# A two-layer mixture-of-experts kernel: five of eight batches stored among the last sparse tiles, sums pinned behind the last output, eight output buffers, and an end in program order

## The chip, the cores and the metric

The kernel runs on one core of a Trainium2 chip, as one program and one launch. The metric is the device time in microseconds (us). Before the change it is 367.66 us, the median of three runs (367.42 to 375.38).

One core has a matrix engine (TensorE, "PE" in the profile; its weight loads are listed apart as "PEld"), a vector engine (VectorE, "DVE"), an engine for activation functions (ScalarE, "ACT"), GpSimd ("POOL"), and SyncE ("SP"), which here does nothing but issue DMAs and wait. Each engine has its own stream of instructions and runs it in order; engines wait for each other at semaphores. DMAs can be issued from SyncE, ScalarE and GpSimd, and their packets are moved by sixteen DMA engines.

## The reference

The input `x` is 8 batches of 256 tokens with 128 features, in f32. Two layers run on it, each with a residual:

```python
x = x + L0_ffn(L0_cond(x, ..., prompt_type))    # pooling, then 8 experts, dense
x = x + L1_ffn(L1_cond(x, ..., language))       # adapter, then top 2 of 8 experts
```

`L0_cond` gives every position an attention-pooled sum over its batch: scores are `tanh(x W1 + b1) . v`, masked by one of three masks that depend on the batch's prompt type, and then a softmax. `L0_ffn` runs all eight experts on every token (128 to 512, gelu with tanh, back to 128) and sums them with gates; a gate is the logit where it is at least the 3072nd smallest of all logits, and else 0.

`L1_cond` is a small adapter per language (128 to 32, relu, back), a residual, and a layer norm with a scale and shift per language. `L1_ffn` is the part that matters here:

```python
xn = layernorm(x) * gamma + beta
probs = softmax(xn @ gate_w)                     # 8 experts
w, idx = top_k(probs, 2);  w = w / sum(w)
out_e = gelu(xn @ w1[e] + b1[e]) @ w2[e] + b2[e] # 128 -> 512 -> 128
return sum_e(w_e * out_e) + x                    # two experts per token
```

So every token has exactly two rows of expert output, and the result of a token is its residual plus these two rows.

## The kernel before

**Tiles.** The 2048 tokens are 16 token tiles of 128 (two for each batch), in four groups of four. The work is cut into five units (`UNITS`): units 0 to 2 have four token tiles each, units 3 and 4 two each.

**The dense layer.** `layer("first", ...)` runs unit by unit and expert by expert: first matmuls (L784), gelu on ScalarE (L786), second matmuls (L764), gating and accumulation on VectorE (L752, L754). Its weights `w10` lie in a pool called `first` under the tag `w1`, with eight buffers; its second weights `w20` lie in the pool `const`. Between matmuls, `pump()` advances generators, which write the other work's instructions in among them.

**Routing.** When a unit's dense layer is finished, its `adapt(u)` is put behind as such a generator. It computes the adapter and norms, keeps the residual in `resid`, picks the two experts of each token, and counts rows by expert through two small matmuls with the constant `ones` and a triangle (`kp`). From these it takes each row's position, and GpSimd writes each token's normalized row, together with its destination number and its weight, twice into a scratch tensor `xs` in device memory by an indirect DMA (L676). In `xs` every expert has a region of its own, so each expert's rows lie one behind the other.

**Lists.** After units 2, 3 and 4 (`SLOTS = {2: 17, 3: 21, 4: 39}`) VectorE turns the counts into a list of 128-row tiles: `tiles_of` (how many tiles each expert has: full ones, at the end also the begun ones), `cumulated` and `listed` (for slot k: which expert, and which row of `xs`). `used` remembers how many tiles of each expert were already listed, and the list of the next unit goes on from there. Slots 0 to 16 come from the first list, 17 to 20 from the second, 21 to 38 from the third. Which rows are in which tile depends on the data, so the kernel learns the tile's start and expert from the list at run time.

**The sparse layer.** For each slot k there are four steps:

- `fetch`: SyncE reads the slot's row and expert from the list into registers, and loads the 128 rows `xt` from `xs` (L814) and the expert's first weights `wt`, 256 KB (L822).
- `turn`: TensorE transposes (L829), VectorE scales (`xc`, L831) and copies the expert's bias (`b1`, L833).
- `hidden`: four matmuls (L840) and four gelus on ScalarE (L842) into `hs`, in a ring of 15 buffers under the tag `scr`.
- `output`: four matmuls (L849), bias on VectorE into `yt` (L852, four buffers), the row's weight on ScalarE (L853), and on GpSimd an indirect DMA of the 128 rows into the second scratch tensor `ys` (L854), to the destination that each row carries.

The steps of different slots overlap: fetches run five slots ahead (`LEAD`), the others two (`AHEAD`). Slots up to `SURE` = 36 always run; slots 36 to 38 stand under a `tc.If` on the count of tiles (L903 to L905), and were not taken in the profiled execution.

**The end** (L906 to L916). Row numbers in `ys` are `(p n t s)`: partition, batch, half of the batch's tokens, first or second expert. Each batch's rows, 256 KB, are read back, alternately from SyncE's and ScalarE's queue; VectorE adds the first row to the residual and the second to that; and the sum is stored, 128 KB for each batch, from the same two queues:

```python
for n in range(B):
    yg.append(work.tile([P, 2, 2 * D], F32, tag="scr", name=f"yg{n}", bufs=NSCR))
    (nc.scalar if n % 2 else nc.sync).dma_start(out=yg[n], in_=yv[n])
for n in range(B):
    ...
    nc.vector.tensor_tensor(o, yg[n][:, :, :D], resid[...], ALU.add)
    nc.vector.tensor_tensor(o, o, yg[n][:, :, D:], ALU.add)
    (nc.scalar if n % 2 else nc.sync).dma_start(out=of[n], in_=...)
```

**What sets the order.** The framework's scheduler orders the instructions of each engine, with the place in the program as priority, and puts in the waits between engines from what reads and writes the same buffer or tensor. Where the program knows better, it says so: `declare_no_dep` with a named group takes away the dependence of one DMA on a group of others, as the output scatters have among themselves. No such thing is said of the scatters and the reads of the end, so every read of `ys` stands behind every scatter.

Of the kernel before, what the change touches and what calls it, by code (L numbers as in the profile page):

```python
# [22 lines left out]
P = 128  # L23
# [19 lines left out]
SURE = 36  # L43
NOWHERE = 1 << 20
# [24 lines left out]
def tile_adaln_ffn_d2(ctx: ExitStack, tc: tile.TileContext, x, ptype, lang, cols, b1v,  # L69
# [36 lines left out]
    for e in range(E):  # L106
        t = first.tile([P, HC * P], F32, tag="w1", name=f"w10_{e}")
        nc.sync.dma_start(out=t, in_=w10[e])
        w10s.append(t)
        t = const.tile([P, HC, D], F32, name=f"w20_{e}")  # L110
        nc.sync.dma_start(out=t, in_=w20[e])
        w20s.append(t)
# [5 lines left out]
    nc.gpsimd.memset(ones, 1.0)  # L118
# [242 lines left out]
    nc.gpsimd.iota(dest, pattern=[[1, 2], [2, NT]], base=0, channel_multiplier=2 * NT)  # L361
# [140 lines left out]
    used = const.tile([P, E], F32, name="used")  # L502
    nc.gpsimd.memset(used, 0.0)
# [15 lines left out]
    def cumulated(f, name):  # L519
        c3 = small.tile([P, E, E], F32, tag="c3", name=f"c3_{name}", bufs=2)  # L520
        nc.vector.tensor_tensor(c3, upto, f.unsqueeze(1).to_broadcast([P, E, E]), ALU.mult)
        cf = small.tile([P, E], F32, tag="cf", name=f"cf_{name}")
        nc.vector.tensor_reduce(cf, c3, AX.X, ALU.add)
        return cf

    def tiles_of(counts, edges, name):

        c2 = small.tile([P, E, NT], F32, tag="c2", name=f"c2_{name}", bufs=2)
        nc.vector.tensor_tensor(c2, counts.unsqueeze(2).to_broadcast([P, E, NT]),
                                edges.unsqueeze(1).to_broadcast([P, E, NT]), ALU.is_ge)  # L530
        f = small.tile([P, E], F32, tag="f", name=f"nf_{name}")
# [3 lines left out]
    def listed(f, cf, first, k0, k1, name):  # L535
# [3 lines left out]
        shape = [P, n, E]  # L539
        past = small.tile(shape, F32, tag="past", name=f"past_{name}", bufs=1)  # L540
        nc.vector.tensor_tensor(past, kth[:, :n].unsqueeze(2).to_broadcast(shape),
                                cf.unsqueeze(1).to_broadcast(shape), ALU.is_ge)
        ek = small.tile([P, n], F32, tag="ek", name=f"ek_{name}", bufs=1)
        nc.vector.tensor_reduce(ek, past, AX.X, ALU.add)

        step = small.tile([P, E], F32, tag="step", name=f"step_{name}", bufs=1)
        if first is None:
            nc.vector.tensor_copy(step, f)
        else:
            nc.vector.tensor_tensor(step[:, :E - 1], first[:, :E - 1], first[:, 1:], ALU.subtract)  # L550
            nc.vector.tensor_copy(step[:, E - 1:], first[:, E - 1:])
            nc.vector.tensor_tensor(step, step, f, ALU.add)
# [4 lines left out]
        if first is not None:  # L557
            nc.vector.tensor_scalar(row, row, first[:, 0:1], None, ALU.add)  # L558
# [7 lines left out]
    def adapt(u, acc):  # L566
# [99 lines left out]
        if u in SLOTS:  # L666
            counts = small.tile([P, E], F32, tag="counts", name=f"counts{u}", bufs=2)
            nc.vector.tensor_copy(counts, kp[:, nt, :])
        for s, oh in enumerate((oh1, oh2)):
# [17 lines left out]
        if u in SLOTS:  # L687
# [3 lines left out]
            if lists:  # L691
# [275 lines left out]
```

## Time and profile before

The profile is of one execution. It took 380.68 us, with a span of 379.0 us from its first to its last instruction and a mean granted TensorE clock of 0.977 of full speed; the median of the three runs without profile is 367.66 us.

| | busy us | share of span | instructions |
|---|---|---|---|
| PE (matmuls) | 345.8 | 91% | 1596 |
| PEld (weight loads) | 233.0 | 61% | 1596 |
| DVE | 195.0 | 51% | 801 |
| ACT | 167.0 | 44% | 387 |
| POOL | 94.5 | 25% | 142 |

DMA moved 46.12 MB in 33,603 packets, 122 GB/s over the span.

The dense layer's matmuls (L784 and L764) take 241.8 us of PE's 345.8, the sparse layer's (L840 and L849) 78.8. The profile names groups by source line, by the program's tile names (`ys<-yt,xt` is a scatter of outputs, `yg<-ys` a read at the end, `xt<-xs` and `wt<-in_w_dram` the fetches) and by shape. A row of the timeline gives the start of a stretch, its length, the engine, the line and tiles, the number of instructions in it, and in brackets how long the engine had been idle before it and what it waited for. "SPq" and "ACTq" are the sequencers that issue DMAs. In the profile's page the span is also cut into 40 slices of 9.5 us, and each digit is the busy share of a slice in tenths.

### The profile page before, as it was taken

How to read it: one execution, taken by the hardware profiler on the slowest of the kernel's cores; microseconds unless marked ns; L12 is line 12 of the kernel's file. 1: busy time of each engine (PE TensorE's matmuls, PEld its weight loads, DVE VectorE, ACT ScalarE, POOL GpSimd, SP SyncE). 2: the span in 40 equal slices, each digit the busy share in tenths (PEclk: the TensorE clock that was granted, in tenths of full speed). 3: DMA queues.
4: the chain of work that ended last, by engine and by line, in shares of the span. 5: the costliest groups of instructions: out<-in, count | busy, mean ns of one | idle time of the engine just before them, and what ended most of it. 6: DMA issues, size and time to landing. Idle time of an engine off the chain costs nothing. (4 is left out here: it accounts for less than half of the span.)

```text
span 379.0 us, 5911 instructions
## 1 busy us (share of the span) xinstructions
PE 345.8 (91%) x1596; PEld 233.0 (61%) x1596; DVE 195.0 (51%) x801; ACT 167.0 (44%) x387; POOL 94.5 (25%) x142
## 2 busy tenths in 40 slices
PE   6799999999999999999999999989989879999900
PEld 6695444444444445445445688857869769999900
DVE  4775565542245675565512474847576644333305
ACT  2166434553542244223443244425635637567800
POOL 8100000000000030650350021262045565444530
PEclk9999999999999999999999999999999998999975
DMA  6935999005222101210130001126543554566136
GB/s 189 382 84 150 368 379 356 4 0 148 69 77 102 56 30 55 63 49 30 56 69 14 28 29 42 36 65 175 151 121 107 162 162 121 168 187 173 47 117 244
DMA packets 33603, 46.12 MB, mean 122 GB/s; under 512 B 5349, under 2 KB 16375, under 8 KB 33569
## 3 DMA queue, kind: packets, MB, share of 16 engines
q1 hardware_dynamic: 29024, 39.26, 34.6%
q0 software_dynamic: 2304, 4.37, 3.2%
q10 hardware_dynamic: 2240, 2.10, 1.6%
q8 instruction: 14, 0.23, 0.3%
q14 instruction: 21, 0.16, 0.1%
HBM read 31.57 MB, written 14.39 MB: 121 GB/s over the span
## 5 line engine op out<-in xcount | busy, mean ns | idle before, releaser
L786 ACT ACTIVATE hT_first<-hp_first,col 128x512 f32<-128x512 f32 (+1 forms) x160 | 93.4, 601 | 103.3 <-PE hp_first L784 102.3
L784 PE MATMUL hp_first<-poolT,w 128*128 128x512 f32 (+1 forms) x320 | 121.2, 513 | 1.3 <-DVE xr L591 0.7
L764 PE MATMUL yp_first<-hT_first,w 128*128 128x512 f32 (+1 forms) x320 | 120.6, 511 | 0.0
L784 PEld LDWEIGHTS hp_first<-poolT,w 128*128 128x128 f32 x320 | 58.8, 190 | 44.2 <-issue 38.2
L764 PEld LDWEIGHTS yp_first<-hT_first,w 128*128 128x128 f32 x320 | 59.0, 190 | 42.5 <-issue 38.6
L676 POOL DMA_INDIRECT xs<-zr,pos x32 | 31.5, 986 | 64.3 <-DVE pos L674 27.9
L842 ACT ACTIVATE hs<-hps,b 128x128 f32<-128x128 f32 x144 | 40.6, 365 | 11.2 <-PE hps L840 5.3
L854 POOL DMA_INDIRECT ys<-yt,xt x36 | 35.2, 977 | 40.9 <-ACT hs L842 28.3
L849 PE MATMUL yps<-w,hs 128*128 x288 | 39.6, 283 | 2.5 <-DVE row L558 2.4
L840 PE MATMUL hps<-xc,wt 128*128 128x128 f32 x288 | 39.2, 280 | 1.1 <-issue 1.1
L849 PEld LDWEIGHTS yps<-w,hs 128*128 128x128 f32 x288 | 35.7, 195 | 4.3 <-issue 3.5
L752 DVE SCALAR_TENSOR_TENSOR part_first<-yp_first,col,gbc_first 128x512 f32<-128x512 f32 (+1 forms) x28 | 17.2, 614 | 40.4 <-PE yp_first L764 39.9
L840 PEld LDWEIGHTS hps<-xc,wt 128*128 128x128 f32 x288 | 36.0, 196 | 0.8 <-issue 0.6
L853 ACT ACTIVATE yt<-yt,xt 128x128 f32<-128x128 f32 x36 | 14.6, 405 | 23.3 <-issue 15.0
L754 DVE TENSOR_TENSOR acc_first<-acc_first,part_first 128x512 f32<-128x512 f32 (+1 forms) x35 | 20.1, 580 | 0.5
L579 POOL MEMSET ha<- 1x512 f32 x5 | 2.6, 516 | 67.6 <-PE dp L588 67.4
L406 POOL DMA_DIRECT2D gd_L<-gT_L x1 | 0.6, 649 | 74.3 <-DVE gT_L L404 74.3
L833 DVE COPY b<-col 128x4 f32 x36 | 7.2, 200 | 23.0 <-ACT hs L842 17.7
L852 DVE TENSOR_TENSOR yt<-yps,b2all 128x128 f32<-128x128 f32 x36 | 10.5, 291 | 14.8 <-PE yps L849 7.1
L831 DVE TENSOR_SCALAR xc<-xtp,col 128x128 f32<-128x128 f32 x36 | 14.4, 401 | 4.0 <-PE xtp L829 2.4
L772 ACT ACTIVATE y_first<-yp_first,col 128x512 f32<-128x512 f32 x8 | 5.5, 687 | 24.2 <-PE yp_first L764 24.2
L420 DVE TENSOR_SCALAR_CACHE_REDUCE fl<-logit,tr 128x128 f32<-128x128 f32 x46 | 13.5, 343 | 0.6
(205 smaller groups left out, 304.2 us busy)
## 6 DMA issues: line engine op xcount, KB each, us to landing
wt<-in_w_dram SPq DMA_DIRECT2D x36, 256.0 KB
xs<-empty SPq DMA_DIRECT2D x1, 8580.0 KB
w<-in_w_dram SPq DMA_DIRECT2D x24, 256.0 KB
gbc_first<-gd_L SPq DMA_DIRECT2D x24, 256.0 KB
xt<-xs SPq DMA_DIRECT2D x36, 65.0 KB
gbc_first<-gd_L SPq DMA_DIRECT2D x16, 128.0 KB
lgb<-in_lgb_dram SPq DMA_DIRECT2D x8, 128.0 KB
yg<-ys ACTq DMA_DIRECT2D x4, 256.0 KB
```

The costliest lines, as they stand in the source:

```text
L676: move = nc.gpsimd.indirect_dma_start(out=xs, out_offset=bass.IndirectOffsetOnAxis(ap=pos[:, t:t + 1], axis=0), in_=zr[s][:, t, :], in_off ...
L752: nc.vector.scalar_tensor_tensor(part, y, bias, gbc, ALU.add, ALU.mult)
L754: nc.vector.tensor_tensor(accs[u], accs[u], part, ALU.add)
L764: nc.tensor.matmul(yp, lhsT=w2s[e][:, c, :], rhs=hT[:, c, :], start=(c == 0), stop=(c == HC - 1))
L784: nc.tensor.matmul(hp, lhsT=w1s[e][:, c * P:(c + 1) * P], rhs=sources[g][:, o * P:o * P + n], start=True, stop=True)
L786: nc.scalar.activation(hT[:, c, :], hp, act, bias=col[:, cb1 + e * HC + c:cb1 + e * HC + c + 1])
L831: nc.vector.tensor_scalar(xc, tp, col[:, C_LG:C_LG + 1], col[:, C_LB:C_LB + 1], ALU.mult, ALU.add)
L840: nc.tensor.matmul(hp[:, c, :], lhsT=wt[:, c * P:(c + 1) * P], rhs=xc, start=True, stop=True)
L842: nc.scalar.activation(hT[:, c, :], hp[:, c, :], AF.Gelu, bias=b1[:, c:c + 1])
L849: nc.tensor.matmul(yp, lhsT=hT[:, c, :], rhs=w21[:, bass.ds(ek, 1), c * D:(c + 1) * D], start=(c == 0), stop=(c == HC - 1))
L853: nc.scalar.activation(yt, yt, AF.Copy, scale=xt[:, D + 1:D + 2])
L854: move = nc.gpsimd.indirect_dma_start(out=ys, out_offset=bass.IndirectOffsetOnAxis(ap=xt.bitcast(I32)[:, D:D + 1], axis=0), in_=yt, in_off ...
```

## The change

1. **Five early batches.** Batches 0 to 4 (`EARLY = 5`) are the tokens of token tiles 0 to 9. At unit 2 VectorE also counts, for every expert, how many tiles hold at least one row of these ten token tiles (`holding`). Each list now has two classes, and lists the tiles up to `holding` first and the others after them. The arrays by expert (`f2`, `at2`, `new`, `cf`, `past`, `step`) are 16 wide instead of 8, and `listed` loses its special case for the first list.
2. **Reads among the last tiles.** With `SETTLED = 21 + 8 = 29`, the output step of slot 28 is followed in the program by five reads of batches 0 to 4 on SyncE's queue, into `scr` buffers. The scatters from slot 29 on are declared independent of these reads.
3. **Row order in `ys`.** Rows are numbered batch by batch, `(n p t s)` instead of `(p n t s)`, so `dest` and the view `yv` change.
4. **Output buffers.** The second dense weights `w20` move from the pool `const` to the pool `first`, tag `w2`, with eight buffers; `yt` takes its buffers from that tag, so it has eight instead of four.
5. **The end.** The drain of the last slots, the sums of the five early batches (in place into `resid`), the register reads of the count and the `tc.If` stand under a manual schedule for VectorE, ScalarE and GpSimd, that is, in program order. Behind the `tc.If`, batches 5 to 7 are read as six halves, alternately on the two queues; then the five early batches are stored; then each half is added and stored. Adds and stores are kept in program order.
6. The constant `ones` is set by VectorE instead of GpSimd.

```diff
+EARLY = 5
+SETTLED = SLOTS[NU - 2] + E
...
-        t = const.tile([P, HC, D], F32, name=f"w20_{e}")
+        t = first.tile([P, HC, D], F32, tag="w2", name=f"w20_{e}")
...
-    nc.gpsimd.memset(ones, 1.0)
+    nc.vector.memset(ones, 1.0)
...
-    nc.gpsimd.iota(dest, pattern=[[1, 2], [2, NT]], base=0, channel_multiplier=2 * NT)
+    nc.gpsimd.iota(dest.rearrange("p s (n t) -> p s n t", t=2), pattern=[[1, 2], [4 * P, B], [2, 2]], base=0,
+                   channel_multiplier=4)
...
     def cumulated(f, name):
-        c3 = small.tile([P, E, E], F32, tag="c3", name=f"c3_{name}", bufs=2)
-        nc.vector.tensor_tensor(c3, upto, f.unsqueeze(1).to_broadcast([P, E, E]), ALU.mult)
-        cf = small.tile([P, E], F32, tag="cf", name=f"cf_{name}")
+        shape = [P, 2, E, E]
+        c3 = small.tile(shape, F32, tag="c3", name=f"c3_{name}", bufs=1)
+        nc.vector.tensor_tensor(c3, upto.unsqueeze(1).to_broadcast(shape), f.unsqueeze(2).to_broadcast(shape), ALU.mult)
+        cf = small.tile([P, 2, E], F32, tag="cf", name=f"cf_{name}", bufs=2)
         nc.vector.tensor_reduce(cf, c3, AX.X, ALU.add)
+        nc.vector.tensor_scalar(cf[:, 1, :], cf[:, 1, :], cf[:, 0, E - 1:], None, ALU.add)
         return cf
...
-        shape = [P, n, E]
+        shape = [P, n, 2 * E]
...
         nc.vector.tensor_reduce(ek, past, AX.X, ALU.add)
...
+        nc.vector.scalar_tensor_tensor(ek, past[:, :, E - 1], -float(E), ek, ALU.mult, ALU.add)
...
+        if t0 < 2 * EARLY <= t0 + nt:
+
+            some = small.tile([P, E], F32, tag="some", name="some", bufs=1)
+            nc.vector.tensor_copy(some, kp[:, 2 * EARLY - t0, :])
+            tiles_of(some, begun, "some", holding)
...
-            if lists:
-                nc.vector.tensor_tensor(f, f, used, ALU.subtract)
-            cf = cumulated(f, str(u))
-            lists[u] = listed(f, cf, used if lists else None, k0, k1, str(u))
+
+            at2, f2, new = (small.tile([P, 2, E], F32, tag=t, name=f"{t}{u}", bufs=1) for t in ("at2", "f2", "new"))
+            nc.vector.tensor_copy(at2[:, 0, :], used)
+            nc.vector.tensor_tensor(at2[:, 1, :], f, holding, ALU.min)
+            nc.vector.tensor_tensor(at2[:, 1, :], at2[:, 1, :], used, ALU.max)
+            nc.vector.tensor_tensor(f2[:, 0, :], at2[:, 1, :], used, ALU.subtract)
+            nc.vector.tensor_tensor(f2[:, 1, :], f, at2[:, 1, :], ALU.subtract)
+            cf = cumulated(f2, str(u))
+            lists[u] = listed(f2, cf, at2, k0, k1, str(u))
...
-                nc.vector.tensor_tensor(new, new, f, ALU.min)
-                nc.vector.tensor_tensor(used, used, new, ALU.add)
+                nc.vector.tensor_tensor(new, new, f2, ALU.min)
+                for i in range(2):
+                    nc.vector.tensor_tensor(used, used, new[:, i, :], ALU.add)
...
-        yt = work.tile([P, D], F32, tag="yt", name=f"yt{k}", bufs=4)
+
+        yt = first.tile([P, HC, D], F32, tag="w2", name=f"yt{k}")[:, 0, :]
...
+        if k >= SETTLED:
+            tc.declare_no_dep(move.ins, group="settled", reason="no more outputs for the first batches")
+        if k == SETTLED - 1:
+            for n in range(EARLY):
+                load(n, slice(0, 2), nc.sync, "settled")
+
+
+    yv = ys.rearrange("(n p t s) d -> n p t (s d)", n=B, t=2, s=2)
+    of = out.rearrange("b (p u) d -> b p u d", u=2)
+    loaded = deque()
+
+    def load(n, part, queue, group=None):
+        y = work.tile([P, 2, 2 * D], F32, tag="scr", name=f"yg{n}_{part.start}", bufs=NSCR)[:, part, :]
+        move = queue.dma_start(out=y, in_=yv[n, :, part, :])
+        if group:
+            tc.add_to_no_dep_group(group, move.ins)
+        loaded.append((n, part, y))
+
+    def add():
+        n, part, y = loaded.popleft()
+        o = resid[n // 2][:, n % 2 * 2 + part.start:n % 2 * 2 + part.stop, :]
+
+        tc.keep_in_program_order(nc.vector.tensor_tensor(o, y[:, :, :D], o, ALU.add))
+        tc.keep_in_program_order(nc.vector.tensor_tensor(o, o, y[:, :, D:], ALU.add))
+        return n, part, o
+
+    def store(queue, n, part, o):
+        tc.keep_in_program_order(queue.dma_start(out=of[n][:, part, :], in_=o))
...
+    ending = ExitStack()
+    ending.enter_context(tc.manual_schedule(engines={DVE, ACT, POOL}))
     while flipped or hid:
         proceed(0)
     while behind:
         pump()
+    sums = [add() for _ in range(EARLY)]
...
+    ending.close()
+    queues = itertools.cycle((nc.sync, nc.scalar))
+    for n in range(EARLY, B):
+        for t in range(2):
+            load(n, slice(t, t + 1), next(queues))
+    for done_sum in sums:
+        store(next(queues), *done_sum)
+    while loaded:
+        store(next(queues), *add())
```

## The prediction

> **What bounds the kernel now.** I read the page first, then the last chain in order of time, SyncE's own waits, the timeline from 350 us, and busy time by stretch.
>
> ```profile
> span 379.0 us, 5911 instructions
> PE   6799999999999999999999999989989879999900
> DMA  6935999005222101210130001126543554566136
> ```
>
> TensorE is full from the third slice to the 38th; the last two slices (19 us) have none of it. While it is busy, only a faster TensorE stage helps; behind it every microsecond counts. The change works on the end, so I followed the chain there (start, length, what):
>
> ```profile
> 362.64 2.46 DMA ys<-yt,xt
> ...
> 365.18 0.34 SPq L911
> ...
> 366.39 6.65 DMA yg<-ys
> ...
> 374.60 0.67 DVE o L914 x2
> 375.27 0.33 DVE o L915
> ```
>
> The last scatter lands at 365.1. Only then are all eight batches (256 KB each, 2 MB) read back, added on VectorE and stored. The wait of SyncE's queue, and the timeline, say how long this had been pending:
>
> ```profile
> SPq L911 <- DMA ys<-yt,xt: 13.9, 1, 13.9
> ```
>
> ```profile
> 351.92 0.97 POOL L854 DMA_INDIRECT ys<-yt,xt  x1 [1.07 <-ACT hs L842]
> ...
> 365.18 2.29 SPq L911 DMA_DIRECT2D yg<-ys  x4
> 369.43 0.76 DVE L914 TENSOR_TENSOR o<-yg,resid 128x256 f32<-128x256 f32 x2 [7.49 <-DMA yg<-ys]
> 371.38 0.76 DVE L914 TENSOR_TENSOR o<-yg,resid 128x256 f32<-128x256 f32 x2 [0.52 <-DMA yg<-ys]
> 373.16 0.76 DVE L914 TENSOR_TENSOR o<-yg,resid 128x256 f32<-128x256 f32 x2 [0.35 <-DMA yg<-ys]
> ```
>
> SyncE has nothing else to do for 13.9 us. The scatter at 351.92 is the eighth from the end, that of tile 28. Its data moves between 353.4 and 353.7 (the software queue's packets in that stretch). Adds start as each pair of batches lands: 4.25, 6.20 and 7.98 us after 365.18. From 365.18 to the end are 13.8 us.
>
> ```profile
> 304.00:306.00 2.00, 2.00 (x21) 2.00 (x20) 1.59 (x13) 1.22 (x5) 1.34 (x2) 1.00 0.65 168
> 306.00:308.00 2.00, 2.00 (x21) 2.00 (x19) 1.77 (x10) 0.53 (x2) 1.57 (x2) 1.00 0.67 217
> 310.00:312.00 2.00, 0.27 (x1) 0.19 (x1) 0.00 (x0) 0.00 (x0) 1.38 (x2) 1.00 0.40 69
> 352.00:360.00 8.00, 7.96 (x69) 7.65 (x68) 1.88 (x7) 6.73 (x25) 4.80 (x6) 1.00 0.07 24
> 366.00:379.00 13.00, 0.00 (x0) 0.00 (x0) 5.63 (x16) 0.00 (x0) 0.00 (x0) 0.50 0.72 243
> ```
>
> (Length, then busy time of PE, PEld, DVE, ACT, POOL, clock, DMA share, GB/s.) From 352 to 360 the DMA engines are 7% busy, and from 366 on 72%: a hole beside a crowd. At 304 to 308 VectorE is 80 to 89% busy. At 310 to 312 PE, DVE and ACT stand almost still together, as VectorE and ScalarE do at 328 to 330. This execution took 380.68 us (span 379.0, 1.7 around it), 13.0 above the median of 367.66; such stops may be part of that. After 365 I see none, so I carry the saving in microseconds to the median.
>
> **The tail.** Five batches are read behind tile 28. Release: landing near 354.0 (351.92 plus the 2.1 to 2.5 us that scatters take here). SyncE's last fetch is issued at 349.2, and the new reads stand behind it in program order; behind them on SyncE is only the count's register read, needed at 365. Five issues at the old 0.57 us take 2.9 us, and 1.3 MB at the measured 243 GB/s 5.4 us: all in by about 361.5, in the hole. The five sums cost ten adds; a pair of batches took 1.43 us (369.43 to 370.86), so 3.6 us. They stand behind the last output's add (361.64 to 361.94) and end at about 365.5, while the last scatter lands. Cost nothing; if the hole were closed, 3.6 us would return.
>
> Left behind the last scatter: three batches in six halves, three issues on each of two queues (0.44 us each on ScalarE's), 0.79 MB. The ring has 15 scratch buffers, and counted through it the third to sixth half fall on those of batches 0 to 3, so they wait for these sums as well: near 364.8, just ahead of 365.1. In the trace 0.5 MB had landed after 4.25 us and 1.0 MB after 6.20, so 0.79 MB after 5.2; the trace's semaphore records put the third and fourth transfers at 5.4 and 6.1, and I take 5.5. Two adds on a half: 0.5 us (128x128 adds in the outputs take 0.29 each, overlapped). The five early stores (0.64 MB) go out behind the reads; at the 390 GB/s of 369 to 372 they take 1.6 us and are through before the last half's store needs the queue. Add 0.3 for stores that take turns. From the issue of the last store to the end took 3.0 us (375.96 to 379.0), kept. Sum: 5.5 + 0.5 + 0.3 + 3.0 = 9.3 against 13.8: **4.5 us saved**.
>
> Here a rule speaks against the halves. The Trainium skill ("DMA: Bandwidth & Descriptors", section "Bandwidth") says to batch transfers to 1 MiB, with 138 GB/s at 64 KB and 341 at 1 MB. My estimate from that page: 170 GB/s at 128 KB, so 0.79 MB in 4.6 us, plus 0.9 us to the first packet and 0.7 for the completion (both from the trace): 6.2 rather than 5.5, and a saving of 3.8. The row shows several transfers in flight running at 390 GB/s together, so I keep 5.5; 4.9 to 6.5 are its ends. Batch-major rows in the scratch tensor make each read contiguous; the trace has no such read: from 0.5 faster (the first microseconds of the old reads ran at 100 to 200 GB/s) to 0.5 slower, taken as zero.
>
> **Sums beside the last scatters.** The same skill ("SBUF — State Buffer", section "Who interferes with whom") warns that a VectorE instruction with two SBUF inputs blocks a GpSimd one that reads SBUF. By the rule the ten adds could hold the last scatter's descriptors for up to 3.6 us. The nearest row: adds with both inputs in SBUF (L754, L571) ran at 278.4 and 278.8 beside scatters of 0.96 and 0.98 us, and the 36 output scatters spread only from 969 to 1041 ns. I take 0.1; ends 0 and 1.
>
> **Lists.** More VectorE work per list. Small operations take 0.16 us, about 0.2 with the step between; the 18-slot arrays go from 144 to 288 elements (0.30, and 0.42 for 256, so 0.44; four of them: +0.56); the 64-element pair doubles (+0.12). List after unit 2: 11 small (2.2) + 0.7 + the new count (0.15 + 0.28 + 0.28) = 3.6. After unit 3: 7 small, 1.4 + 0.3 = 1.7. Last: 6 small, 1.2 + 0.7 = 1.9. Together 7.2 us. Latency is covered: after the first list SyncE still waits 6.5 us for scattered rows; the second ends at 281.84 and is read at 301.83; the last is read at 314.98, but that fetch then waits 2.2 us more for an old scatter. The new count stands ahead of unit 2's positions, so these scatters start 0.7 later, and their first turn is at 274.9, 16 us after the rows arrive. What isn't covered is VectorE's own time where it paces the tiles: 274 to 278 (3.79 of 4 us busy) and 303 to 308. Of the 3.6 us that fall there I charge 0.6; ends 0 and 3.6.
>
> **At nothing.** Eight output buffers in the freed second-layer weights: the waits of L852 in the drain end with TensorE, and the scatter four tiles back had landed; 0, at best 0.3. `ones` on VectorE: idle from 2.6 to 6.1 us there. Program order at the end: these outputs already run in that order, and GpSimd's count read ahead of the last scatter costs 0.2 at most; 0 to -0.2.
>
> Sum: -4.5 + 0.1 + 0.6 = -3.8. In the profile's terms 375.2 of span; on the median **363.9 us**.
>
> **Rivals.**
> *A, the forecast*, 62%: 361.9 to 366.
> *B, the sparse pace rises too*, 13%. From 333.58 to 351.92 outputs come every 2.04 us, while TensorE needs 17 matmuls at 0.111 = 1.89. The timeline shows a ring: gelu, bias copy L833, L852, L853, gelu. Some 14 tiles at 0.15 give 2.1, and outputs now trail TensorE by 2.5 us. If the new buffers or order open the ring: 363.9 - 2.1 = 361.8, with the trailing gone 359.3. Against it: the bias copy's buffers are untouched.
> *C, the early reads do not come early*, 12%: they wait for all scatters, or a buffer. Then 2 MB is read at the end as now and only the halves help by about 0.5: 367.2. Against it: the row lists take the early batches first, and later scatters are declared independent.
> *D, the lists' VectorE work lands on the tiles' path*, 13%, the slower side. All 7.2 us paid: -4.5 + 7.2 = +2.7, 370.4. It decides at 4.5 us. For: VectorE is the busiest follower at 274 and 304. Against: half of it (3.6 us) is the list of unit 2, where TensorE has queued work.
>
> **Numbers.** The range 360.2 to 368.0 takes A and C, the upper part of B and the start of D. About 2% (7.4 us) is what a measurement here can tell from no change. Faster by more: the end of B and a lucky A, 12%; slower by more than that: 4%; within: 84%.
>
> **What would show it.** Five reads issued at 354 to 357 and the stretch 352 to 360 well above 7% DMA; ten adds right behind the last L852; about 0.8 MB read after the last landing and about 9 us from there to the end. Wrong if these reads appear after the last scatter, if scatters beside the adds exceed 1.1 us, or if TensorE idles near 275 or 305 behind L541 to L562.

## The result, and the profile after

The changed kernel takes 0.9956 of the time before, with a 95% interval of 0.994 to 0.9971 (21 runs of each, medians 367.23 and 368.39 us). By the ratio that is 1.6 us less, with 1.1 to 2.2 for the interval; the forecast was 3.8. A second comparison, in another set of runs, gave 0.9942 (0.9916 to 0.9969). The direction was right, but 1.6 of the forecast 3.8 us arrived.

Some executions take some 6 us longer (in one, the first profile of the changed kernel, the dense layer begins at 36.10 us instead of 30.26); the ratio leaves them out, and the medians do not. The first profile of the kernel before was 13 us over its median. So both were profiled a second time, and those profiles are compared here. In them the first dense matmul starts at 30.20 us (before) and 30.26 us (changed), so their times can be laid side by side. The executions took 368.47 and 367.66 us.

The page of the changed kernel, with the same rows as before: span, and the 40 slices of TensorE and of the DMA engines.

```profile
span 365.9 us, 5944 instructions
PE   6899999999999999999999999999999989989940
DMA  7933999201613410021122001113564365677446
```

The hole in the DMA row near the end is filled. Busy time by stretch (length, then PE, PEld, DVE, ACT, POOL, clock, DMA share, GB/s), for the eight microseconds behind tile 28's scatter and for the end:

```profile
344.00:352.00 8.00, 7.76 (x70) 7.57 (x68) 1.98 (x7) 6.76 (x25) 4.65 (x6) 1.00 0.58 187
358.00:365.90 7.90, 0.00 (x0) 0.00 (x0) 3.14 (x12) 0.00 (x0) 0.00 (x0) 0.50 0.72 227
```

The first stretch was 7% busy in the profile that the prediction read; it is now 58%. The chain that ended last, first in the second profile of the kernel before, then in the changed one:

```profile
341.05 12.29 DMA ys<-yt,xt x2
...
354.62 6.21 DMA yg<-ys
...
363.06 0.33 DVE o L915
```

```profile
343.41 13.10 DMA ys<-yt,xt x2
...
356.64 0.32 SPq L890
...
357.53 4.06 DMA yg<-ys
...
362.47 0.29 DVE resid L900
```

In each, the first line ends with the landing of the last scatter: 353.34 us before, 356.50 changed (343.41 + 13.10, less what the rounding adds). From there to the end are 13.4 us before and 9.4 changed, where 13.8 and 9.3 were forecast. So the end did what it should. But the landing itself is 3.2 us later, and that is what ate the rest. The timeline of the changed kernel shows the end in detail:

```profile
343.41 0.97 POOL L872 DMA_INDIRECT ys<-yt,xt  x1 [1.07 <-ACT yt L871]
...
346.34 11.67 SPq L890 DMA_DIRECT2D yg<-ys  x8
...
352.00 0.41 DVE L899 TENSOR_TENSOR resid<-yg,resid 128x256 f32<-128x256 f32 x1
...
352.88 1.18 POOL L872 DMA_INDIRECT ys<-yt,xt  x1 [0.30 <-DVE resid L900]
...
359.30 0.29 DVE L899 TENSOR_TENSOR resid<-yg,resid 128x128 f32<-128x128 f32 x1 [3.23 <-DMA yg<-ys]
```

Tile 28's scatter starts at 343.41, the first early read is issued at 346.34, and the first early sum starts at 352.00 without waiting for its data. One scatter beside the sums takes 1.18 us instead of 0.97. The first add of a half starts 2.7 us after the first issue behind the landing. SyncE's wait for scatters in front of the reads was 12.8 us at one time before; it is now cut in two, with the early reads between (9.9 us in total, 2 times, the longest 5.3):

```profile
SPq L890 <- DMA ys<-yt,xt: 9.9, 2, 5.3
```

The table counts from the first dense matmul. It is taken from instruction starts in the two second profiles.

| us from the first dense matmul to | before | changed | difference |
|---|---|---|---|
| x2T of the last unit (VectorE) | 246.55 | 248.02 | +1.5 |
| last count matmul of the last unit (kp, TensorE) | 268.89 | 271.84 | +3.0 |
| output scatter of tile 10 (GpSimd) | 278.10 | 280.42 | +2.3 |
| output scatter of tile 28 | 310.84 | 313.15 | +2.3 |
| output scatter of tile 35, the last | 321.00 | 324.11 | +3.1 |
| end | 336.55 | 335.68 | -0.9 |

Thus 2.3 us are lost before tile 10, nothing between tiles 10 and 28, another 0.8 us from tile 28 to the last, and 4.0 us are won behind that. (These single executions differ by 0.9; the timed runs say 1.6 and 2.1.)

**Where the 2.3 us arise.** VectorE, in the routing of the last unit, before:

```profile
276.76 0.41 DVE L571 TENSOR_TENSOR x2T<-acc_first,xT 128x256 f32<-128x256 f32 x1
...
294.56 0.17 DVE L631 COPY lg<-l1p 128x16 f32<-128x16 f32 x1
...
298.26 0.42 DVE L653 TENSOR_TENSOR sofar<-sofar,sel 128x8 f32<-128x8 f32 x2
```

and changed:

```profile
277.92 0.21 DVE L721 TENSOR_TENSOR new<-new,f 128x16 f32<-128x16 f32 x1
278.01 0.20 DVE L563 TENSOR_REDUCE row<-past 128x4 f32<-128x64 f32 x1
278.19 0.17 DVE L723 TENSOR_TENSOR used<-used,new 128x8 f32<-128x8 f32 x1
278.28 0.42 DVE L578 TENSOR_TENSOR x2T<-acc_first,xT 128x256 f32<-128x256 f32 x1
...
296.04 0.17 DVE L638 COPY lg<-l1p 128x16 f32<-128x16 f32 x1
...
297.73 0.17 DVE L850 COPY b<-col 128x4 f32 x1 [1.11 <-ACT hs L859]
297.81 0.17 DVE L493 TENSOR_TENSOR s_p<-s_p,rank 128x16 f32<-128x16 f32 x1
...
301.26 0.42 DVE L660 TENSOR_TENSOR sofar<-sofar,sel 128x8 f32<-128x8 f32 x2
```

In both kernels instructions of the list after unit 3 stand on VectorE among those in front of x2T, the first step of the last unit's adapter; with the longer list (`new`, `row`, `used`) x2T is 1.5 us late. The delay stays constant to the logits (`lg`, 1.5). Then a second 1.5 us is added before `sofar`: in the new order of VectorE's instructions a tile's bias copy, which waits 1.11 us for a gelu, stands in the middle of the search for the two experts.

What waits for these positions is GpSimd. Before, and then changed:

```profile
300.68 0.98 POOL L854 DMA_INDIRECT ys<-yt,xt  x1 [1.42 <-DVE wh L671]
301.96 0.96 POOL L676 DMA_INDIRECT xs<-zr,pos  x1 [0.30 <-DVE cf L523]
...
305.76 0.96 POOL L676 DMA_INDIRECT xs<-zr,pos  x1 [0.30 <-issue]
307.02 0.98 POOL L854 DMA_INDIRECT ys<-yt,xt  x1 [0.31 <-issue]
```

```profile
301.29 0.96 POOL L872 DMA_INDIRECT ys<-yt,xt  x1 [1.43 <-ACT hs L859]
303.93 0.96 POOL L688 DMA_INDIRECT xs<-zr,pos  x1 [1.68 <-issue]
...
306.46 1.22 POOL L872 DMA_INDIRECT ys<-yt,xt  x1 [0.30 <-issue]
...
309.41 0.96 POOL L688 DMA_INDIRECT xs<-zr,pos  x1 [0.30 <-issue]
```

The last unit's four scatters (`xs<-zr,pos`) stand in GpSimd's order among the outputs' scatters. From them on GpSimd issues scatters without a gap longer than 0.35 us, one every 1.28 us but for two long ones, until about 315 (before) and beyond 320 (changed). SyncE's fetches wait for these scatters. The fetch of tile 21 is the first from the last list:

```profile
SPq L831 <- DMA xs<-zr,pos: 2.3, 1, 2.3
```

In the changed kernel it waits these 2.3 us until the last unit's rows have landed in `xs`, then 0.6 us more until tile 10's scatter gives back its row buffer, and is issued 1.9 us later than before, where its waits were under 0.3 us. So the late start of this queue passes on to the tiles behind it. The profiles agree: the scatter of tile 28 comes 32.5 to 33.3 us behind that of tile 10 in thirteen of the fourteen that were taken at this pace with three lists (32.7 before, 32.7 and 33.3 in the two of the changed kernel), and 33.7 in the other, whatever was done to the lists.

GpSimd's queue is not the only way, though. TensorE runs its own instructions in order, and the adapter's first matmul (`adp`, which needs x2T) stands among those of the tiles. Before, and then changed:

```profile
277.22 0.62 PE L581 MATMUL adp<-x2T,lw 128*32 128x256 f32 x2
```

```profile
279.28 0.62 PE L588 MATMUL adp<-x2T,lw 128*32 128x256 f32 x2
...
301.74 0.40 PE L666 MATMUL kp<-sofar,ones 128*128 128x24 f32 x2 [1.21 <-DVE sofar L660]
...
320.90 0.30 PE L846 MATMUL xtp<-ident,xt 128*128 128x128 f32 x1 [0.72 <-DMA xt<-xs]
```

The transposition of a tile on TensorE is 1.5 us late from tile 5 on, right behind `adp`, and 1.8 us from tile 14 on, behind the count matmuls (TensorE waits 1.21 us for them, 0.87 before). It is 2.3 us late from tile 24 on, after TensorE has waited 0.72 and 0.47 us for rows that the late fetches bring (0.50 us at one time before). So the late routing reaches the tiles twice, through TensorE's order and through GpSimd's queue, by about the same amount; no run takes one way away and leaves the other.

### The profile page after: what moved, and what is told of

It is laid out like the page before. It is cut to its first block, busy times and chain, and to the rows that moved or that the text cites. A ratio compares the mean times of both kernels' runs of the same rounds, so it can differ in the third digit from the quotient of the medians.

```text
span 371.8 us, 5944 instructions
## 1 busy us (share of the span) xinstructions
PE 349.5 (94%) x1596; PEld 237.9 (64%) x1596; DVE 198.9 (53%) x835; ACT 166.6 (45%) x387; POOL 95.5 (26%) x141
## 5 line engine op out<-in xcount | busy, mean ns | idle before, releaser
L866 PE MATMUL yps<-w,hs 128*128 x288 | 38.0, 276 | 0.5 <-ACT hs L859 0.5
L857 PE MATMUL hps<-xc,wt 128*128 128x128 f32 x288 | 38.2, 276 | 0.0
L857 PEld LDWEIGHTS hps<-xc,wt 128*128 128x128 f32 x288 | 35.1, 192 | 0.6 <-issue 0.4
```

The source lines that it names most:

```text
L857: nc.tensor.matmul(hp[:, c, :], lhsT=wt[:, c * P:(c + 1) * P], rhs=xc, start=True, stop=True)
L866: nc.tensor.matmul(yp, lhsT=hT[:, c, :], rhs=w21[:, bass.ds(ek, 1), c * D:(c + 1) * D], start=(c == 0), stop=(c == HC - 1))
```

## The experiments

"From the first dense matmul" means the same counting as in the table. Each ratio is to the kernel before, run on the same chip in the same set.

After the first profile the loss had three possible causes: the lists' VectorE work falls on the tiles' path (theory L, the prediction's rival D); the order of ScalarE's instructions in the drain, which had changed (theory O); and the traffic of the early reads beside the last fetches and scatters (theory T). When L had proved right, the question was what of the lists costs: the place of the list after unit 3 in front of the last unit's adapter (P), the last unit's positions and GpSimd's queue behind them (G), or just the amount of work (W). What the lists say, the order of the tiles, changed together with them; no run has the new order without the new work. But x2T is late before TensorE has waited for the rows of any tile of the new order.

### A second look at before, the lists alone, and the early reads left out

The kernel before, unchanged:

> The kernel before, once more, for a second profile of it: the first one ran 13 us over its own median. Both theories expect the last scatter to land 13 to 14 us before the end, as in the first profile. They differ in the stretch from the first dense matmul to that landing. In the profile of the changed kernel it is 326.6 us (36.10 to 362.68). If something in the sparse layer of the changed kernel costs about 3 us (theory S), this stretch is 322 to 324 us here. If the change costs nothing there and the end is shortened by less than the profile says (theory E), it is 326 to 327 us.

Measured: 368.47 us; 323.1 us from the first dense matmul to the last landing (353.34 - 30.20). Something in the sparse layer of the changed kernel costs about 3 us: theory S holds and theory E falls.

The kernel before with the lists of the changed one, its end and its buffers left alone:

```diff
+        nc.vector.tensor_scalar(cf[:, 1, :], cf[:, 1, :], cf[:, 0, E - 1:], None, ALU.add)
...
+            tiles_of(some, begun, "some", holding)
...
+            nc.vector.tensor_tensor(at2[:, 1, :], f, holding, ALU.min)
...
+            lists[u] = listed(f2, cf, at2, k0, k1, str(u))
```

> The kernel before with the two-class lists alone; its end, its row order and its buffers are the old ones. Theory L (the lists' work on VectorE falls on the tiles' path): 1.5 to 3.6 us slower than the kernel before. Theory O: at most 0.6 us slower, the charge of the prediction.

Measured: ratio 1.0047 (1.0014 to 1.008), 1.7 us slower (0.5 to 3.0); in the trace the end is at 339.39 instead of 336.55, 2.8 us later, with x2T at 248.04, the last count matmul at 271.98 and tile 28's scatter at 313.06, as in the changed kernel. The lists alone bring the whole loss in front of tile 28, without any early read (so theory T falls). Their VectorE work is 19.08 us instead of 12.59: 3.1 more after unit 2, 1.5 after unit 3, 1.9 after the last.

The changed kernel with the early reads taken out and put behind the last scatter:

```diff
-        if k == SETTLED - 1:
-            for n in range(EARLY):
-                load(n, slice(0, 2), nc.sync, "settled")
...
-    sums = [add() for _ in range(EARLY)]
...
+    for n in range(EARLY):
+        load(n, slice(0, 2), next(queues))
```

> The changed kernel without the early reads: all five batches are read behind the last scatter too, whole, ahead of the six halves, and everything else stays as changed (lists, row order, eight output buffers, program order at the end). Theory L: 1 to 3 us slower than the kernel before, since the lists stay and the reads return. Theories O and T: within 0.7 us of the kernel before, the halves gaining what the lists cost.

Measured: ratio 1.0069 (1.0033 to 1.0104), 2.5 us slower than before. That is theory L. Against the changed kernel it also gives the worth of the early reads: 340.29 against 335.68 in the traces, 4.6 us.

### Does the changed kernel with the old lists reach the forecast?

```diff
-            lists[u] = listed(f2, cf, at2, k0, k1, str(u))
+            lists[u] = listed(f, cf, used if lists else None, k0, k1, str(u))
...
-        move = queue.dma_start(out=y, in_=yv[n, :, part, :])
+        flat = xs.rearrange("r c -> (r c)")[n * P * 4 * D:(n + 1) * P * 4 * D]
+        move = queue.dma_start(out=y, in_=flat.rearrange("(p t d) -> p t d", p=P, t=2))
```

> The changed kernel with the single-class lists of the kernel before. Since the early batches are then not complete at tile 28, the five early reads take as many bytes from the sparse input instead, at the same time (behind the scatters up to tile 28) and in the same shape: the first five batches of the output are not the reference's, all else is done. Theory L (the lists are the whole loss): the forecast's sum without its charge for the lists, 3.5 to 4.5 us faster than the kernel before, ratio 0.988 to 0.9905. If the order on ScalarE or the traffic of the early reads takes a good part: 2 to 3 us faster, 0.992 to 0.9945.

The changed kernel itself, beside it:

> The changed kernel itself, beside the others on their chip: 0.9956 of the kernel before, as measured, which is 1.6 us.

Measured: ratio 0.9837, but with a wide interval (0.9763 to 0.991, few runs). The traces, of one execution each, have 333.12 us from the first dense matmul to the end, against 336.55 before and 335.68 changed. So the change saves 3.4 us with the old lists and 0.9 with the two-class ones: these cost 2.6. GpSimd's queue is back where it was:

```profile
301.81 0.96 POOL L682 DMA_INDIRECT xs<-zr,pos  x1 [0.30 <-DVE cf L529]
...
306.88 0.98 POOL L861 DMA_INDIRECT ys<-yt,xt  x1 [0.30 <-ACT yt L860]
308.17 0.98 POOL L861 DMA_INDIRECT ys<-yt,xt  x1 [0.31 <-issue]
```

Tile 9's output scatter is at 306.88 here and at 307.02 before. (The first dense matmul is at 30.1 here.) The forecast without its charge for the lists was 4.4. The missing microsecond has the size of what the drain takes longer (11.2 us from tile 28's scatter to the last, 10.2 before); but giving part of the drain back (the last of these experiments) did not give back the time.

### Does the cost of list work depend on its place?

Nine VectorE operations in series, which multiply the tile counts by 1, in the kernel before; after unit 3, after unit 2, and in the last list:

```diff
             f = tiles_of(counts, begun if u == NU - 1 else full, str(u))
+            for _ in range(9 if u == 3 else 0):
+                nc.vector.tensor_scalar(f, f, 1.0, None, ALU.mult)
```

> The kernel before with nine more VectorE operations of 0.16 us in the list after unit 3 (each multiplies the tile counts by 1), 1.5 us in series. Theory P (place: this list stands on VectorE in front of the first step of the last unit's adapter, x2T, and the adapter is followed by the last positions, the last scatters and the last list): x2T of the last unit starts 1 to 1.5 us later than the 246.6 us behind the first dense matmul that it has before, and the end is 1 to 1.5 us later. Theory W (only the work counts, wherever it stands; 6.5 us cost 2.9): 0.7 us later, as in the run with the same operations after unit 2.

> The same nine operations in the list after unit 2, where SyncE waits for scattered rows after it has read the list, and TensorE has dense work queued. Theory P: less than 0.3 us later. Theory W: 0.7 us.

> The kernel before, with the same nine operations in the last list, that is, behind the last positions. Theory G: less than 0.3 us later, since the fetches that read this list are held by the scatters four us longer than the list takes. Theory W: 0.7 us.

Measured: after unit 3, ratio 1.0034 (1.0018 to 1.0051) and 1.75 us later in the trace, the last count matmul 1.2 later. After unit 2, ratio 1.0037 (1.0005 to 1.0068) and 0.6 us later in the trace, the count matmul 0.5 later. In the last list, ratio 0.9979 (0.9955 to 1.0002): nothing. The last list is free, as theory G says; the first two both cost, which P did not expect of unit 2. The times can't tell those two apart, only the traces do. x2T moved by just 0.6 us in the run after unit 3, so the padding reached the positions on other ways too.

The same padding in the last unit's routing, in front of the count matmuls:

```diff
         last[0] = sofar[:, nt, :]
+        for _ in range(9 if u == NU - 1 else 0):
+            nc.vector.tensor_scalar(sofar[:, nt, :], sofar[:, nt, :], 1.0, None, ALU.mult)
```

> The kernel before, with nine VectorE operations of 0.16 us in series in the last unit's routing, right ahead of the matmuls of its counts (kp, L659), so that its positions come 1.5 us later; no list is touched. Theory G (what counts is when the last unit's positions come: its four scatters into the sparse input stand in GpSimd's order ahead of the outputs' scatters, GpSimd then has a queue of them back to back, and the fetches wait for those to give back the buffers of the rows): 1 to 1.5 us later at the end, and the scatter of tile 28 as much later. Theory W (6.5 us of VectorE work cost 2.9 wherever it stands): 0.7 us.

Measured: 383.13 and 383.40 us in the two executions (of four) that can be compared, against a median of 381.4 for the kernel before, with no interval: some 1.8 us later. The direction is theory G's, the size is not settled. This run, the padding in the last list and two more runs below were made on a chip on which every kernel took some 13 us longer.

### Can the lists' cost be bought back?

The list after unit 3 behind the first additions of the last unit's adapter:

```diff
+        if postponed:
+            enlist(NU - 2, postponed.pop())
+            done.add("list 3")
+            yield
```

> The changed kernel, with the list after unit 3 written in the program behind the first additions of the last unit's adapter instead of ahead of it; same operations, same number. Theory P: x2T of the last unit returns to 246.6 us or earlier behind the first dense matmul (248.0 in the changed kernel), and the kernel is 1 to 2 us faster than the changed kernel, 364.4 to 365.4 where the kernel before has 367.6. Theory W: the same as the changed kernel.

Measured: x2T is back at 246.27, but the last count matmul is at 271.49 (271.8 changed): the step from x2T to the adapter's sum takes 1.0 us longer than before, the next to the transposes 0.9, the last from the logits to the counts 1.1. The work had moved inside the same chain. Ratio 0.9947 (0.9916 to 0.9977), not to be told from the changed kernel. Theory P falls in its narrow form: x2T is not the place that counts.

The same list behind the last positions:

> The changed kernel, with the list after unit 3 moved behind the last unit's positions, just ahead of the last list: none of its 5.8 us of VectorE work lies in the last unit's routing any more. Theory G: the matmuls of the last unit's counts start at 269 us or earlier behind the first dense matmul (268.9 before, 271.8 in the changed kernel), tile 28's scatter at 311 to 312 (313.6 changed), and the kernel is 1.5 to 2.5 us faster than the changed kernel, 364 to 365 where the kernel before has 367.6. Theory W: the same as the changed kernel. If the list now comes too late for the fetch of tile 17, which is issued near 270 us, that fetch moves instead and part of the gain is gone.

Measured, on the slower chip: 0.9952 (0.9927 to 0.9977), again the changed kernel's ratio. Its count matmuls are not back: 275.24, where the first profile of before, which ran at that chip's pace, has 273.42.

No list after unit 3 at all, 22 slots from the last list, early reads from tile 26 on:

```diff
-SLOTS = {2: 17, 3: 21, 4: 39}
+SLOTS = {2: 17, 3: 17, 4: 39}
...
-SETTLED = SLOTS[NU - 2] + E
+SETTLED = 2 * 2 * EARLY + E - 1
```

> The changed kernel without a list after unit 3: slots 17 to 38 come from the last list, which has the early tiles first, so that 27 slots settle the first five batches; the early reads follow tile 26, in buffers of their own. It has 5.8 us less VectorE work than the changed kernel and 4.3 less than lists of the kernel before had in that place. Theory G (the last unit's positions): their matmuls kp start at 269 us or earlier behind the first dense matmul, and the kernel is 2 to 3.5 us faster than the changed kernel, ratio 0.986 to 0.990 to the kernel before. If the last list comes too late for the fetch of tile 17, TensorE stands for 3 to 5 us near 285 us behind the first dense matmul, and the kernel is slower than the changed one.

Measured: ratio 1.0098 (1.0065 to 1.0131), 3.6 us slower than before. The last list ends at 281.40, too late for the fetch of tile 17, and tile 20's scatter comes at 303.75 instead of 294.55. The count matmul is at 271.86, no earlier. So the kernel is better with the third list than without.

The same two-class lists from fewer operations (the row in three instead of five, merged updates, no copy of the used tiles, the count of early tiles behind unit 2's positions):

```diff
-        nc.vector.tensor_tensor(row, kth[:, :n], row, ALU.subtract)
-        nc.vector.tensor_scalar(row, row, fl[:, 0:1], None, ALU.add)
-        nc.vector.tensor_scalar(row, row, float(P), None, ALU.mult)
+        nc.vector.scalar_tensor_tensor(row, row, fl[:, 0:1], kth[:, :n], ALU.subtract, ALU.subtract)
```

> The changed kernel with the same two-class lists from fewer operations: in each list the row needs three operations instead of five, the update of the used tiles two fewer after units 2 and 3 by merged ones, no copy of the used tiles, and the count of early tiles stands behind unit 2's positions. That is 3 to 5 operations of 0.15 to 0.2 us fewer in each list. By the padding's slopes (0.4 us per us after unit 2, 1.2 after unit 3): 0.7 to 1.2 us faster than the changed kernel, ratio 0.991 to 0.9935 to the kernel before, 334.4 to 335.0 us from the first dense matmul to the end (335.7 changed). If the cost comes from the order of VectorE's instructions and not from their amount, it can be anything from 0 to 2.6.

Measured: VectorE's list work falls by 1.6 us (17.44), but the last count matmul comes at 272.45, later than in the changed kernel, and the ratio is 0.9989 (0.997 to 1.0008). Expected was 0.991 to 0.9935. So the amount of work alone is not the measure. Every one of these kernels has its own order on VectorE, and each that ran at the usual pace loses 2.6 to 3.6 us up to the count matmuls, at other steps of the same chain. How much of the 2.6 us is work and how much is order stays open.

### The order on ScalarE in the drain

In the changed kernel the buffers of the five early reads come from the ring of `hs`, between those of tiles 30 and 31. ScalarE's order there is no longer that of the kernel before. Before:

```profile
340.37 0.40 ACT L853 ACTIVATE yt<-yt,xt 128x128 f32<-128x128 f32 x1 [0.61 <-ACT hs L842]
340.68 1.12 ACT L842 ACTIVATE hs<-hps,b 128x128 f32<-128x128 f32 x4
341.68 0.41 ACT L853 ACTIVATE yt<-yt,xt 128x128 f32<-128x128 f32 x1
```

Changed:

```profile
342.73 0.40 ACT L871 ACTIVATE yt<-yt,xt 128x128 f32<-128x128 f32 x1 [0.61 <-ACT hs L859]
343.36 0.40 ACT L871 ACTIVATE yt<-yt,xt 128x128 f32<-128x128 f32 x1 [0.23 <-DVE yt L870]
344.92 0.40 ACT L871 ACTIVATE yt<-yt,xt 128x128 f32<-128x128 f32 x1 [1.15 <-DVE yt L870]
345.22 3.18 ACT L859 ACTIVATE hs<-hps,b 128x128 f32<-128x128 f32 x12
```

Three output scales, the last of which waits 1.15 us, stand in front of twelve gelus; behind them GpSimd has a gap of 2.04 us between the scatters of tiles 30 and 31. The order is the same in every profile of a kernel, so it is fixed when the program is built. It is the old one in the run without early reads, which keeps the eight output buffers and the manual schedule, and the new one in all five kernels whose early reads take buffers of the ring. So the ring makes the difference. The runs below give the reads other buffers (and the outputs four again), and the old order returns:

```diff
-        yt = first.tile([P, HC, D], F32, tag="w2", name=f"yt{k}")[:, 0, :]
+        yt = work.tile([P, D], F32, tag="yt", name=f"yt{k}", bufs=4)
...
-        y = work.tile([P, 2, 2 * D], F32, tag="scr", ...)[:, part, :]
+        pool, tag, more = (first, "w2", {}) if group else (work, "scr", {"bufs": NSCR})
+        y = pool.tile([P, 2, 2 * D], F32, tag=tag, ...)[:, part, :]
```

This was run on four kernels and, on the slower chip, on a fifth (with the list after unit 3 behind the last positions):

> The changed kernel, with the five early reads in buffers of their own (the freed second-layer weights, which the outputs give back) instead of in the ring of hs. This puts the gelus of tiles 31 to 33 back ahead of the output scales of tiles 29 and 30 on ScalarE, as in the kernel before. Theory O (the order on ScalarE costs time: gelu 31 ran 1.6 us after its matmuls in the changed kernel): 1.2 to 2 us faster than the changed kernel, 364.4 to 365.2 where the kernel before has 367.6. Theory T (the traffic of the early reads beside the last fetches and scatters costs it) and theory L (the lists cost it): the same as the changed kernel, 366.0 to 366.4.

> The same (old lists, early reads from the sparse input, the first five batches of the output not the reference's), and the early reads in buffers of their own, which restores the order on ScalarE. Theory O (that order costs time in the drain): 0.5 to 1.2 us faster than the run before this one. Otherwise the same as that.

> The list after unit 3 moved as in the run before, and the early reads in buffers of their own, so that ScalarE keeps the order of the kernel before. If both causes are real and add up: 2 to 3.5 us faster than the changed kernel, 363 to 364.4 where the kernel before has 367.6. If the order on ScalarE costs nothing: no faster than the run with the list moved alone.

> The same, with the early reads in buffers of their own, so that ScalarE keeps the old order in the drain. By the pairs run so far (335.1 against 335.7, and 333.4 against 333.1): within 0.6 us of the run before this one.

> The same list order, and the early reads in buffers of their own, which restores the order on ScalarE in the drain. Theories G and O together: 0.5 to 1.5 us faster than the run with the list moved alone, 363 to 364.5 where the kernel before has 367.6. If the order on ScalarE is hidden behind GpSimd's scatters: no faster than that run.

| | tile 28's scatter to the last, us: reads in the ring | apart | end, ring | end, apart | ratio, ring | ratio, apart |
|---|---|---|---|---|---|---|
| changed | 11.0 | 10.5 | 335.68 | 335.12 | 0.9956 and 0.9942 | 0.9972 (0.9921 to 1.0024) |
| old lists | 11.2 | 10.6 | 333.12 | 333.42 | 0.9837 | 0.9824 (0.9732 to 0.9917) |
| list 3 moved | 11.2 | 10.1 | 335.04 | 335.32 | 0.9947 | 0.9932 (0.9906 to 0.9957) |
| fewer operations | 11.6 | 10.1 | 336.89 | 335.48 | 0.9989 (0.997 to 1.0008) | 0.9947 (0.9926 to 0.9967) |

In all four pairs the drain is shorter, by 0.5 to 1.5 us (10.2 in the kernel before, 9.9 with the early reads left out). The end follows in two of the pairs and not in the others, where tile 28's scatter itself came 0.6 and 1.3 us later; only the pair with fewer operations shows it in the times. On the slower chip, too, it gave nothing: 0.9966 (0.9943 to 0.9989) against 0.9952. So theory O's 1.2 to 2 us did not come: the order costs 0.5 to 1.5 us in the drain (0.8 between the kernel before and the changed one), of which on the average of these pairs 0.3 to 0.4 reaches the end, within the spread of the single traces.

No version run here beats the changed kernel clearly. The lowest ratio with the full output is the one with list 3 moved and the reads' buffers apart, 0.9932 (0.9906 to 0.9957).

## Why the prediction was wrong: right in the tail, wrong in the lists

**The tail** (forecast -4.5): right. From the last landing to the end 13.4 us became 9.4, and 9.1 in the first profile of the changed kernel, where 9.3 was worked out. The parts fit as well: the six halves and their adds take 6.3 us (5.5 + 0.5 forecast), the last store and the end 3.1 (0.3 + 3.0). The first half's add starts 2.7 us after the first issue, and from there the adds follow each other at 0.5 to 0.7 us a half, with the transfers just ahead of them: the fifth half lands at 361.59, 5.1 us behind the last scatter, and the sixth by 362.15 at the latest, 5.7. The estimate from the rule against small transfers was 6.2; the one from the trace's row, 5.5, was nearer.

**Sums beside the last scatters** (forecast +0.1): right. One scatter took 1.18 us instead of 0.97, which passes the stated sign of being wrong (1.1) at a cost of 0.2; where no sums stand beside them (before, lists alone, no early reads), none from tile 28 on takes over 0.98. The 3.6 us that the prediction worked out from the rule did not come. The sums took 4.1 us where 3.6 was forecast, and ended in front of the last landing.

**Output buffers** (forecast 0): in agreement, though no run has the four buffers alone: the kernels with four buffers, and the reads apart, are no slower than those with eight. The batch-major rows were not tried alone either.

**Lists** (forecast +0.6, ends 0 and 3.6): this is the step that failed. The work was sized well, 6.5 us against 7.2. What failed is "latency is covered": it asked who reads each list, and when, and found slack at every reading. It did not ask what stands behind the list on VectorE. Behind the list after unit 3 stands the whole routing of the last unit, x2T to positions, and behind the positions stands GpSimd's queue. The row that could have said so was on the table: the fetch that reads the last list "waits 2.2 us more for an old scatter". The next question, what makes that scatter late, leads to GpSimd, back to back at 1.28 us, and from there to the positions that start its queue. The prediction did see VectorE full at 274 to 278, just ahead of x2T (3.79 of 4 us), and charged 0.6 of the 3.6 us that fall there and at 303 to 308, without a row for that share; it thought of the pace of the tiles, not of the routing. The measured term is 2.3 to 2.8 us in the traces (1.7, 0.5 to 3.0, in the timed runs of the lists alone), inside the stated ends, but far from the value taken. Its sign, TensorE idle behind L541 to L562, looked at the lists themselves; TensorE waited behind the routing (1.21 us at `kp`). Rival D named the right mechanism and asked for all 7.2 us; about a third came.

**Program order at the end** (forecast 0 to 0.2 gained): the sentence "these outputs already run in that order" was wrong for the changed kernel, and here too a term was put at nothing. It was not the manual schedule that moved ScalarE's order but the ring that the early reads' buffers share with `hs`; the drain grew by 0.8 us.

**Rivals B and C** did not come: outputs between tiles 20 and 28 come every 2.04 us in both kernels (scatters of tiles 27 and 28 at 341.37 and 343.41), and the early reads do come early.

The sum with the measured terms: -4.0 for the tail, +2.3 in front of tile 10, +0.8 in the drain: -0.9 in these traces. The timed runs have -1.6 (-1.1 to -2.2); the 0.7 between them stays open.

## What to carry to other kernels

When added work seems hidden because its result is read late, follow also the engine it runs on: what stands behind it in that engine's order, and which queue in turn waits for that. A buffer taken from a ring that the main loop uses can change the built order of instructions on another engine, so compare the order of every engine before costing a change at nothing. Fewer operations are not a gain as such where the order is set by a scheduler; the profile of the result decides.

## What the runs showed of the hardware

- A queue of indirect scatters on GpSimd, each of 128 rows, goes at one per 1.28 us: 0.97 us of work and 0.30 us between. In the two second profiles this queue lasts 15 us (12 scatters, before) and 18 us (14, changed).
- The list operations on 64 elements take 0.20 us. A VectorE instruction that waits for another engine (the bias copy, 1.11 us for a gelu) holds those that stand behind it: `s_p` starts only at 297.81.
- Sets of runs differ more than the change is worth: the kernel before had medians of 368.39, 369.24, 369.34, 369.52 and 369.20 us in five sets, and 381.98 in the sixth, which was the only one on its chip. Ratios from one set are comparable (0.9952 there, for the list after unit 3 behind the last positions; 0.9956 elsewhere, for the changed kernel), times are not. The first profile of the kernel before, with 380.68 us, has the length of that sixth set; why is not known.
